# A hand-ordered delta-rule layer: its first four slots become an opening of their own

## The chip, the cores and the metric

The kernel runs on one core of one Trainium2 chip. The metric is the device time of one execution in microseconds (us); lower is better. Times given for a kernel are medians over several executions. The profile comes from one execution with the hardware profiler. The engines are called PE (TensorE, matmuls), ACT (ScalarE), DVE (VectorE), POOL (GpSimd) and SP (SyncE; here it issues nearly all DMAs).

## The reference

One layer in fp32 over 4 sequences of 1024 tokens with 512 features: a gated delta-rule attention with 16 heads of 128 by 128, and a mixture of experts (2 of 6 for each sequence, chosen by the sequence's mean). Both stand behind a layer norm and are added to their input.

```python
q = _l2norm(silu(short_conv(h @ Wq))) * SCALE      # conv over 4 tokens, per feature
k = _l2norm(silu(short_conv(h @ Wk)))
v = silu(short_conv(h @ Wv))
g = -exp(A_log) * softplus(h @ Wf1 @ Wf2 + dt_bias)   # 8 decay groups per head
beta = sigmoid(h @ Wb)

def step(S, inp):
    qt, kt, vt, gt, bt = inp
    S = S * exp(gt)[..., None]
    err = einsum('bhk,bhkv->bhv', kt, S)
    S = S + kt[..., None] * (bt[..., None] * (vt - err))[:, :, None, :]
    return S, einsum('bhk,bhkv->bhv', qt, S)

y = o * silu(h @ Wg + bg);  y = y * rsqrt(mean(y * y) + EPS) * norm_w
x = x + y @ Wo
x = x + moe(layernorm(x))
```

## The kernel before

**Tiling.** A sequence is cut into 4 blocks of 256 tokens (index j), a block into 2 chunks of 128; the 16 heads into 4 groups of 4. A *slot* is one sequence, head group and block: 64 slots, n = 16 b + 4 hg + j, of some 80 us each. A *unit* is one chunk of a slot. The recurrence is done by chunks: products of keys and queries inside a chunk, the inverse of a triangular matrix, then a chain over chunks that carries the state.

**The pieces of work.** They are Python generators; every `yield` ends a step.

- `norms(b, j)`: loads the block's two chunks of x (`xl`, L256), normalizes them (DVE `bn_stats`, POOL `rstd` L225/L226, DVE `xn` L227), transposes them on PE (`pt_a` L232) and copies them to `hT` on ACT (L233).
- `decays(b, j)`: PE `pf` (L272), ACT `f1T` (L276), PE `pbeta` (L281), ACT and DVE `beta` (L288 to L290), PE `pg` (L296), then a softplus over ACT and DVE (`gs`, `u`, `w`, L299 to L309) and a product on POOL (`gs`, L313).
- `factors_of(b, j)`: four PE products `px` (L324) of `gs`, each followed by an exponential on ACT into `xs` (L329) and a store of it into `fd` in device memory (L330). After the second and the fourth there is also a column `fgx` (L335), which goes out by four stores into `fg` (L338), one for each head group. At the end `pe` (L342), `xe` (L344) and a store into `fe` (L345). `f1T`, `u`, `w`, `xs` and `xe` share one tag of two buffers.
- `project(...)`: the q, k and v projections of a slot, in two parts of two heads. The weights are loaded with the first part (L358). For each head and each of q, k, v two half pieces of two PE products (`pz`, L400). ACT copies (`z`, L408) and does the first tap of the convolution (L410), DVE the others (L416, nine a head), ACT a Silu (L420).
- `front`: for each unit, loads `fx` from `fd` (L495), `eg` and `fe` (L500, L501), scales keys and queries with them on DVE (`kx` L521 to L532, `kq` L536), products on PE (`pin`, `pmid`, `pout`, L579), transposes (`pt` L620) and norms.
- `gate` (L666 to L675), `inverse` (L693 to L786: `pn` L705, `pxx` L723, `po` up to L782), `chain` (L801 to L845, with `pdl` L806) and `output` (L857 to L864), and for the experts `tokens`, `choose` and `experts`.

**Order.** PE's order is the order in which the program issues its instructions; the scheduler orders the other engines, with a priority for calls under `urgent`. `slot(n)` interleaves the chain of slot n (`c_`), the front of slot n + 1 (`f_`), the inverse of slot n + 1 (`i_`), dense work (`d`: outputs, gates, projections of slot n + 2) and extra work (`e_`) that `also(n, order, generator)` entered for the slot: norms, decays and factors of the coming blocks, and the experts. `fill(k)` takes k steps of the dense work. The twelve steps of the inverse are where `e_` is stepped, two times each, or once in slots with experts.

**The start.** Slots run from `first_slot = -4`; what `also` enters for an earlier slot is put into −4. Slots −4 to −1 have no chain. Slot −3 does the norms, decays and factors of block 0, with nothing beside them; slot −2 all the projections of slot 0, and then the norms, decays and factors of block 1; slot −1 the front of slot 0 (from its third step on), the projections of slot 1, the gate and the inverse of slot 0, and in the inverse's steps the norms, decays and factors of block 2.

A PE queue is worked off in order, so an instruction that waits holds all behind it; so are the queues of the other engines and SP's, where each DMA waits for the data that it stores or for the buffer that it fills.

Of the kernel before, what the change touches and what calls it, by code (L numbers as in the profile page):

```python
# [99 lines left out]
def layer_kernel(  # L100
# [25 lines left out]
    B, T, _ = x.shape  # L126
# [91 lines left out]
    def normed_rows(src, dst, who):  # L218

        st = sp.tile([P, 6], F32, tag="st", name=f"st_{who}")  # L220
        mv = sp.tile([P, 2], F32, tag="mv", name=f"mv_{who}")
        nc.vector.bn_stats(st, src)
        nc.vector.bn_aggr(mv, st)
        rstd = sp.tile([P, 1], F32, tag="rstd", name=f"rstd_{who}")
        nc.gpsimd.tensor_scalar(rstd, mv[:, 1:2], LN_EPS, None, ALU.add)  # L225
        nc.gpsimd.tensor_tensor(rstd, rstd, nhalf[:, :1], ALU.pow)  # L226
        nc.vector.tensor_scalar(dst, src, mv[:, 0:1], rstd[:, 0:1], ALU.subtract, ALU.mult)  # L227

    def transposed(xn, dst, who):
        pt = bank(f"pt_{who}", [P, KC, P])  # L230
        for kc in range(KC):
            nc.tensor.transpose(pt[:, kc, :], xn[:, kc * P : (kc + 1) * P], ident)  # L232
        nc.scalar.copy(dst, pt)  # L233


    def norms(b, j):
        if j == 0:
            seqs[b] = {
                "hT": {},
                "beta": bp.tile([P, NCH, H], F32, tag="beta", name=f"beta_{b}", bufs=2),  # L240


                "fg": dp.tile([NCH, NHG, NG, NH], F32, tag="fg", name=f"fg_{b}"),
                "fd": dp.tile([NCH, GW, NF * P], F32, tag="fd", name=f"fd_{b}"),

                "fe": dp.tile([NCH, P, GW], F32, tag="fe", name=f"fe_{b}"),

                "x1": dp.tile([NCH, P, D], F32, tag="x1", name=f"x1_{b}"),
                "xT": dp.tile([NCH, P, D], F32, tag="xT", name=f"xT_{b}"),
            }  # L250
        Q = seqs[b]
        xns = []
        for cc in range(CPB):
            c = j * CPB + cc
            xl = sp.tile([P, D], F32, tag="xr", name=f"xl_{b}_{c}", bufs=XR)
            nc.sync.dma_start(xl, x[b, c * P : (c + 1) * P, :])  # L256
            xn = sp.tile([P, D], F32, tag="xn", name=f"xn_{b}_{c}", bufs=3)
            normed_rows(xl, xn, f"a{b}_{c}")
            xns.append(xn)
        yield  # L260
        Q["hT"][j] = bp.tile([P, KC, TB], F32, tag="hT", name=f"hT_{b}_{j}", bufs=NBLK)
        for cc in range(CPB):
            transposed(xns[cc], Q["hT"][j][:, :, cc * P : (cc + 1) * P], f"a{b}_{j * CPB + cc}")
            yield

    def decays(b, j):
        Q = seqs[b]
        hT = Q["hT"][j]
        w_ = f"{b}_{j}"
        pf = bank(f"pf_{w_}", [P, TB])  # L270
        for kc in range(KC):
            nc.tensor.matmul(pf, wf1_sb[:, kc, :], hT[:, kc, :], start=(kc == 0), stop=(kc == KC - 1))  # L272
            if kc == 1:
                yield
        f1T = sp.tile([P, TB], F32, tag="xs", name=f"f1T_{w_}")
        nc.scalar.copy(f1T, pf)  # L276
        yield
        pbeta = bank(f"pbeta_{w_}", [P, CPB, H])
        for cc in range(CPB):
            for kc in range(KC):  # L280
                nc.tensor.matmul(  # L281
                    pbeta[:, cc, :], hT[:, kc, cc * P : (cc + 1) * P], wb_sb[:, kc, :],
                    start=(kc == 0), stop=(kc == KC - 1),
                )
            if cc + 1 < CPB:
                yield
        beta = Q["beta"][:, j * CPB : (j + 1) * CPB, :]
        nc.scalar.activation(beta, pbeta, AF.Exp, scale=-1.0)  # L288
        nc.vector.tensor_scalar(beta, beta, 1.0, None, ALU.add)
        nc.vector.reciprocal(beta, beta)  # L290
        yield

        gs = sp.tile([P, CPB, GW], F32, tag="gs", name=f"gs_{w_}", bufs=1)
        pg = bank(f"pg_{w_}", [P, CPB, GW])
        for cc in range(CPB):
            nc.tensor.matmul(  # L296
                pg[:, cc, :], f1T[:, cc * P : (cc + 1) * P], wf2_sb, start=True, stop=True,
            )
        nc.vector.tensor_add(gs, pg, dtb_sb[:, None, :].to_broadcast([P, CPB, GW]))  # L299
        u = sp.tile([P, CPB, GW], F32, tag="xs", name=f"u_{w_}")  # L300
        w = sp.tile([P, CPB, GW], F32, tag="xs", name=f"w_{w_}")
        nc.scalar.activation(u, gs, AF.Abs)
        nc.scalar.activation(u, u, AF.Exp, scale=-1.0)
        nc.vector.tensor_scalar(w, u, 1.0, None, ALU.add)

        nc.vector.scalar_tensor_tensor(u, w, -1.0, u, ALU.add, ALU.subtract)
        nc.scalar.activation(w, w, AF.Ln)
        nc.vector.tensor_sub(w, w, u)
        nc.vector.scalar_tensor_tensor(gs, gs, 0.0, w, ALU.max, ALU.add)  # L309
        gv = gs.rearrange("p c (h g) -> p (c h) g", g=NG)  # L310
        for cc in range(CPB):
            gv = gs[:, cc, :].rearrange("p (h g) -> p h g", g=NG)
            nc.gpsimd.tensor_tensor(gv, gv, nega[:, :, None].to_broadcast([P, H, NG]), ALU.mult)  # L313
        Q["gs"] = gs
        yield
# [732 lines left out]
    prs = [(b, hg, j) for b in range(B) for hg in range(NHG) for j in range(NBLK)]  # L1048
    parts = [list(range(i * NH // CPB, (i + 1) * NH // CPB)) for i in range(CPB)]
    NS = NHG * NBLK  # L1050
    begun = {}
    first_slot = -4
    sparse = set()
    beside = {}

    def also(n, order, g):
        beside.setdefault(max(n, first_slot), []).append((order, g))
# [10 lines left out]

    for b in range(B):
        for j in range(NBLK):  # L1070
            n = NS * b + j
            g = norms(b, j)
            also(n - 3, 1, some(g, 1))
            also(n - 3, 4, idle(2))
            also(n - 3, 5, g)
            also(n - 3, 6, idle(3))
            also(n - 3, 7, decays(b, j))
            also(n - 3, 8, idle(2))
            also(n - 3, 9, factors_of(b, j))
        for c in range(NCH):  # L1080
            also(NS * (b + 1) - NBLK + (c + 1) // 2, 0 if c % 2 else 3, tokens(b, c))
        n = NS * (b + 1) + 1
        also(n, 5, choose(b))
        g = experts(b)
        also(n, 8, some(g, 1))
        for c in range(NCH):
            also(n + 1 + c, 6, some(g, 4 * NFC + 1))
            sparse.add(n + 1 + c)
# [4 lines left out]
    def of(make, n, *k):  # L1093

        if not at(n):
            return iter(())
        b, hg, j = at(n)
        return make(b, hg, 2 * j + k[0]) if k else make(b, hg, j)

    def part(n, i):  # L1100
        return project(*at(n), parts[i]) if at(n) else iter(())

    def dense(n):
# [10 lines left out]
            yield  # L1114
        yield from part(n + 2, 1)

    def slot(n):
        d = dense(n)
        c_ = itertools.chain(of(chain, n, 0), of(chain, n, 1))
        f_ = begun.pop(n + 1, iter(()))  # L1120
        e_ = itertools.chain(*(g for _, g in sorted(beside.pop(n, []), key=lambda x: x[0])))

        def step(g):
            next(g, None)

        def urgent(g):

            with tc.high_priority(URGENT):
                next(g, None)

        def fill(k):
            for _ in range(k):
                next(d, None)

        step(f_)
        urgent(c_)
        fill(2)
        urgent(f_)
        fill(2)
        urgent(c_)  # L1140
        fill(1)
        urgent(f_)
        fill(1)
        urgent(f_)
        urgent(c_)
        fill(1)
        step(f_)
        urgent(c_)
        urgent(f_)
        fill(4)  # L1150
        urgent(c_)
        step(f_)
        fill(4)
        urgent(f_)
        fill(6)
        i_ = of(inverse, n + 1)
        for k in range(12):
            urgent(i_)
            fill(1 if k % 5 in (2, 4) else 2)
            for _ in range(1 if n in sparse else 2):  # L1160
                step(e_)
            if k in (0, 1, 3, 4, 9):
                urgent(c_)
            if k == 2:
                urgent(f_)
            if k == 5 and at(n + 2):
                begun[n + 2] = of(front, n + 2)
            if k in (5, 8) and at(n + 2):
                step(begun[n + 2])
        for g in (c_, f_, i_, d, e_):  # L1170
            for _ in g:
                pass

    with tc.manual_schedule(engines={mybir.EngineType.PE}):
        for n in range(first_slot, max(max(beside), len(prs)) + 1):
            slot(n)


# [46 lines left out]
```

## Time and profile before

| | |
|---|---|
| median of three executions | 5211.04 us (5199.04 to 5218.25) |
| profiled execution | 5219.7 us, its span 5217.9 us |
| mean granted clock of PE | 0.965 |
| PE busy | 4886.8 us, 94% |
| PE busy from 0 to 190 us | 126.05 us, at clock 0.81 |
| PE busy from 190 to 1000 us | 787.16 us, at clock 0.99 |
| DVE, ACT, POOL busy | 69%, 51%, 11% |

The span is the time from the profile's first to its last instruction. A profile line of a timeline reads: start, duration, engine, line of the program, operation, output<-input, shapes, how many instructions are drawn together, and in brackets how long the engine had been idle before and what released it. "PE px L324 <- POOL gs L313: 17.8, 3, 6.7" is a line of the waits: PE, at L324, waited for POOL's `gs` of L313 for 17.8 us in total, 3 times, 6.7 us at most. The windows view gives a stretch of time, its length, the busy time of PE, of its weight loads, of DVE, ACT and POOL with the number of instructions, the granted clock of PE (1.00 is full speed), the busy share of the DMA engines and GB/s.

In the profiled execution PE starts at 12.78 us, when the first `xn` is there. The slots' regular course, with PE nearly without idle time, sets in at some 190 us.

### The profile page before, as it was taken

How to read it: one execution, taken by the hardware profiler on the slowest of the kernel's cores; microseconds unless marked ns; L12 is line 12 of the kernel's file. 1: busy time of each engine (PE TensorE's matmuls, PEld its weight loads, DVE VectorE, ACT ScalarE, POOL GpSimd, SP SyncE). 2: the span in 40 equal slices, each digit the busy share in tenths (PEclk: the TensorE clock that was granted, in tenths of full speed). 3: DMA queues.
4: the chain of work that ended last, by engine and by line, in shares of the span. 5: the costliest groups of instructions: out<-in, count | busy, mean ns of one | idle time of the engine just before them, and what ended most of it. 6: DMA issues, size and time to landing. Idle time of an engine off the chain costs nothing.

```text
span 5217.9 us, 197872 instructions
## 1 busy us (share of the span) xinstructions
PE 4886.8 (94%) x86500; PEld 3683.3 (71%) x86500; DVE 3576.1 (69%) x10397; ACT 2676.3 (51%) x8111; POOL 555.9 (11%) x838
## 2 busy tenths in 40 slices
PE   6899999998899999998889999999888999999988
PEld 4677777776667777776667777777666777777765
DVE  4577878766676776776657667677765776677762
ACT  3445555554455555544455555555454555555531
POOL 1001111111110011101110100101111001001110
PEclk8899999999999999999989999999998999999999
DMA  5233433334344454434334545443533445444322
GB/s 140 64 102 102 108 102 108 100 83 102 98 115 127 116 158 115 128 96 102 100 84 116 137 123 141 121 118 101 118 84 89 127 132 140 128 125 129 82 59 73
DMA packets 333776, 573.01 MB, mean 110 GB/s; under 512 B 90022, under 2 KB 145190, under 8 KB 332908
## 3 DMA queue, kind: packets, MB, share of 16 engines
q1 hardware_dynamic: 332908, 560.34, 40.4%
q8 instruction: 678, 11.11, 1.0%
q14 instruction: 190, 1.56, 0.1%
HBM read 491.01 MB, written 69.22 MB: 107 GB/s over the span
## 4 chain that ended last, share of the span: by engine, by line
PE 68%; DVE 14%; ACT 8%; DMA 5%; issue 3%; POOL 1%; SPq 0%; another core or an unknown queue 0%; POOLq 0%; ACTq 0%; DVEq 0%
PE pz L400 22%; PE pw L860 6%; PE pgt L666 5%; PE ph L1026 3%; PE pn L705 3%; PE pxx L723 3%; PE pfo L1037 3%; PE pin L579 3%; DMA fx<-fd 3%; DVE qkv L416 3%; DMA fd<-xs 2%; DVE kx L527 2%; PE pmid L579 2%; PE pk L801 2%; PE pt L620 2%
## 5 line engine op out<-in xcount | busy, mean ns | idle before, releaser
L416 DVE SCALAR_TENSOR_TENSOR qkv<-z,conv_sb,qkv 128x256 f32<-128x256 f32 x2304 | 1027.2, 486 | 733.9 <-ACT qkv L410 706.8
L527 DVE TENSOR_TENSOR kx<-qkv,fx 128x384 f32<-128x384 f32 x1024 | 541.2, 550 | 68.9 <-ACT qkv L420 48.3
L400 PE MATMUL pz<-hT,wk 128*128 128x256 f32 x2048 | 576.4, 406 | 0.0
L400 PE MATMUL pz<-hT,wv 128*128 128x256 f32 x2048 | 542.6, 393 | 0.0
L860 PE MATMUL pw<-wo,yT 128*128 128x512 f32 x1024 | 517.7, 631 | 24.6 <-ACT xe L344 23.0
L400 PE MATMUL pz<-hT,wq 128*128 128x256 f32 x2048 | 537.8, 396 | 0.6 <-issue 0.6
L666 PE MATMUL pgt<-wg,hT 128*128 128x512 f32 x1024 | 504.3, 605 | 5.2 <-ACT xe L344 5.2
L408 ACT COPY z<-pz 128x512 f32<-128x512 f32 (+1 forms) x512 | 245.8, 480 | 482.2 <-PE pz L400 480.5
L521 DVE TENSOR_TENSOR kx<-qkv,fx 128x128 f32<-128x128 f32 x1792 | 431.8, 284 | 81.2 <-ACT qkv L420 36.3
L579 PE MATMUL pin<-kx 128*32 128x32 f32 x16384 | 408.8, 199 | 38.5 <-DVE U L614 24.0
L400 PEld LDWEIGHTS pz<-hT,wq 128*128 128x128 f32 x2048 | 372.0, 191 | 75.8 <-issue 29.7
L400 PEld LDWEIGHTS pz<-hT,wv 128*128 128x128 f32 x2048 | 369.1, 190 | 79.3 <-issue 21.5
L579 PEld LDWEIGHTS pin<-kx 128*32 128x32 f32 x16384 | 377.6, 112 | 55.1 <-DVE U L614 36.1
L400 PEld LDWEIGHTS pz<-hT,wk 128*128 128x128 f32 x2048 | 374.1, 195 | 52.9
L410 ACT ACTIVATE qkv<-z,conv_sb 128x256 f32<-128x256 f32 x768 | 362.4, 504 | 14.5
L835 ACT ACTIVATE y<-gt 128x128 f32<-128x128 f32 x512 | 157.4, 307 | 391.6 <-DVE gt L816 379.2
L579 PE MATMUL pmid<-qkv 128*32 128x32 f32 x4096 | 343.2, 198 | 14.8 <-issue 14.8
L837 POOL TENSOR_TENSOR ssy<-ssy,nhalf 128x4 f32<-128x4 f32 x128 | 149.7, 1170 | 1929.6 <-DVE ssy L836 1929.6
L579 PE MATMUL pmid<-kx,qkv 128*32 128x32 f32 x4096 | 344.9, 199 | 4.1 <-DVE kx L532 3.4
L536 DVE TENSOR_TENSOR kq<-qkv,fx 128x256 f32<-128x256 f32 x512 | 211.7, 422 | 156.4 <-DMA fx<-fd 82.1
L860 PEld LDWEIGHTS pw<-wo,yT 128*128 128x128 f32 x1024 | 190.6, 201 | 170.3 <-issue 136.8
L420 ACT ACTIVATE qkv<-qkv 128x768 f32<-128x768 f32 x256 | 215.6, 842 | 171.9 <-DVE qkv L416 169.5
(192 smaller groups left out, 10011.8 us busy)
## 6 DMA issues: line engine op xcount, KB each, us to landing
fx<-fd SPq DMA_DIRECT2D x512, 512.0 KB
we<-in_W_dram SPq DMA_DIRECT2D x192, 256.0 KB
x<-xr SPq DMA_DIRECT2D x128, 256.0 KB
xr<-x SPq DMA_DIRECT2D x96, 256.0 KB
we<-in_W_dram SPq DMA_DIRECT2D x96, 192.0 KB
wq<-in_Wq_dram SPq DMA_DIRECT2D x16, 1024.0 KB
wk<-in_Wk_dram SPq DMA_DIRECT2D x16, 1024.0 KB
wv<-in_Wv_dram SPq DMA_DIRECT2D x16, 1024.0 KB
```

The source lines that it names most:

```text
L400: nc.tensor.matmul(pz[:, s - ss_[0], :], weights["w" + "qkv"[s]][:, kc, h * DK : (h + 1) * DK], seqs[b]["hT"][blk][:, kc, :], start=(kc == ...
L408: nc.scalar.copy(z[:, ss_[0] : ss_[-1] + 1, 3:], pz)
L410: nc.scalar.activation(cv[:, s_, :], z[:, s_, 0:TB], AF.Copy, scale=taps[:, s_, 0:1])
L416: nc.vector.scalar_tensor_tensor(cv[:, s, :], z[:, s, k : k + TB], taps[:, s, k : k + 1], cv[:, s, :], ALU.mult, ALU.add,)
L420: nc.scalar.activation(cv, cv, AF.Silu)
L521: nc.vector.tensor_mul(later_half(kx[p][l][:, 0], half), later_half(q, half), later_half(f_[:, :, l, :], half))
L527: nc.vector.tensor_mul(kt[:, :n, 1, hh, :], k[:, hh, None, :].to_broadcast([P, n, P]), f_[:, hh, l0 : l0 + n, :],)
L536: nc.vector.tensor_mul(kq2[:, 2 * p + hh, :, :], qk[:, hh, 0:2, :], f_[:, hh, nl, None, :].to_broadcast([P, 2, P]))
L579: nc.tensor.matmul(o, l_, r_, start=True, stop=True, tile_position=(0, a))
L666: nc.tensor.matmul(pgt, hT[:, kc, c % CPB * P : (c % CPB + 1) * P], weights["wg"][:, kc, :], start=(kc == 0), stop=(kc == KC - 1),)
L835: nc.scalar.activation(y2, y[:, h, :], AF.Square, accum_out=ssy[:, h : h + 1])
L860: nc.tensor.matmul(pw, yT[:, h, :], weights["wo"][:, h, :], start=(h == 0), stop=(h == NH - 1))
```

## The change

Slots −4 to −2 are gone. A new function `opening` does the norms and decays of blocks 0 and 1 and the factors of block 0, and takes one step of slot 0's projections (half a piece: two products) after each of their steps; the rest of the projections follows. The first step of `norms(0, 1)`, which loads x and normalizes, comes before the decays of block 0; the first step of `front` of slot 0, which asks for `fx`, behind the factors of block 0. The slots begin with −1, and the factors of block 1 are entered there, ahead of the extra work for block 2. In slot −1 `fill` also takes a step of the extra work after each step of dense work, so that factors of block 1 and norms, decays and factors of block 2 come earlier than the inverse's steps.

```diff
-    first_slot = -4
+    first_slot = -1
...
     for b in range(B):
         for j in range(NBLK):
+            if b == 0 and j < 2:
+                continue
             n = NS * b + j
...
+    def opening():
+
+        d = itertools.chain(part(0, 0), part(0, 1))
+
+        def with_dense(g, k=1):
+            for _ in g:
+                for _ in range(k):
+                    next(d, None)
+
+        with_dense(norms(0, 0), 0)
+        one = norms(0, 1)
+        next(one)
+        with_dense(decays(0, 0))
+        with_dense(one)
+        with_dense(range(3))
+        with_dense(factors_of(0, 0))
+        begun[0] = of(front, 0)
+        next(begun[0])
+        with_dense(decays(0, 1))
+        with_dense(d)
+        next(begun[0])
+
     def slot(n):
...
         def fill(k):
             for _ in range(k):
                 next(d, None)
+                if n < 0:
+                    step(e_)
...
     with tc.manual_schedule(engines={mybir.EngineType.PE}):
-        for n in range(first_slot, max(max(beside), len(prs)) + 1):
+        opening()
+        also(-1, 0, factors_of(0, 1))
+        for n in range(-1, max(max(beside), len(prs)) + 1):
             slot(n)
```

In the built programs the two PE queues are the same again from the products of unit 2 on (`pout`, `pmid`, `pin` of L579, right behind the last `po` of slot 0's inverse, L782); the queues of ACT, SP and POOL are the same behind the corresponding places, and DVE's has a few neighbours exchanged. ACT's table loads go from 230 to 234. On SP's queue, `xl` of chunk 2 goes ahead of `wq`, and `xl` of chunk 3 ahead of `wk` and `wv`; `wo` and the first `xr` come before the first `fd` store; the two `fx` loads of unit 1's first half stand among the `fd` stores of block 1.

## The prediction

> **What bounds the kernel now.** I read the page's first part, then its chain, then TensorE's waits of the opening, then the timelines that carry them.
>
> ```profile
> PE 4886.8 (94%) x86500; PEld 3683.3 (71%) x86500; DVE 3576.1 (69%) x10397; ACT 2676.3 (51%) x8111; POOL 555.9 (11%) x838
> PE 68%; DVE 14%; ACT 8%; DMA 5%; issue 3%; POOL 1%; SPq 0%; another core or an unknown queue 0%; POOLq 0%; ACTq 0%; DVEq 0%
> ```
>
> TensorE (PE) is busy 94% of the span, so only its idle and half-clock time can be won. The windows view (window, its length, PE busy, the other engines, mean granted PE clock) shows where the opening stands:
>
> ```profile
> 0.00:190.00 190.00, 126.05 (x1576) 95.14 (x1577) 86.69 (x252) 77.24 (x197) 20.41 (x50) 0.81 0.43 111
> 190.00:1000.00 810.00, 787.16 (x15471) 600.62 (x15470) 622.87 (x1797) 413.48 (x1376) 86.28 (x121) 0.99 0.38 100
> ```
>
> Up to 190 us PE idles 64.0 us, and works at clock 0.81; behind it 97% busy at 0.99. Waits of PE up to 175 us (total, times, longest), and the row at 184 us:
>
> ```profile
> PE px L324 <- POOL gs L313: 17.8, 3, 6.7
> PE pf L272 <- ACT hT L233: 13.7, 2, 13.1
> PE pt_a L232 <- DVE xn L227: 12.8, 1, 12.8
> PE pgt L666 <- ACT xe L344: 5.2, 1, 5.2
> PE pn L705 <- DVE xn L698: 5.0, 1, 5.0
> ...
> 184.03 1.33 PE L620 MATMUL pt<-cst,qkv 128*128 128x128 f32 x5 [6.12 <-ACT qkv L420]
> ```
>
> 17.8 + 13.7 + 12.8 + 5.2 + 5.0 + 6.1 = 60.6; four small ones make 3.4 more: the 64.0. The timelines of PE and ACT (start, duration, idle before and its releaser) place them:
>
> ```profile
> 27.39 6.32 PE L324 MATMUL px<-cst,gs 128*128 128x512 f32 x8 [5.98 <-POOL gs L313]
> 54.71 1.04 PE L232 MATMUL pt_a<-cst,xn 128*128 128x128 f32 x8
> 68.80 3.78 PE L272 MATMUL pf<-hT,wf_sb 128*128 128x256 f32 x8 [13.05 <-ACT hT L233]
> 83.51 5.56 PE L324 MATMUL px<-cst,gs 128*128 128x512 f32 x8 [6.66 <-POOL gs L313]
> ...
> 25.48 1.28 ACT L329 ACT_TABLE_LOAD   x1
> 39.89 0.60 ACT L329 ACTIVATE xs<-px 128x512 f32<-128x512 f32 x1 [6.25 <-DMA fd<-xs]
> 45.91 0.38 ACT L344 ACTIVATE xe<-pe 128x256 f32<-128x256 f32 x1 [3.06 <-DMA fd<-xs]
> 101.27 0.38 ACT L344 ACTIVATE xe<-pe 128x256 f32<-128x256 f32 x1 [10.54 <-DMA fd<-xs]
> ```
>
> The reader is to see two kinds of wait. Steps of norms and decays have nothing beside them on PE (5.98, 13.05, 6.66). And `xe` waits for the `fd` store that frees its `xs` buffer, because four tiny `fg` stores (0.1 KB each, L338) stand ahead of it: the DMA records have the first `fg` issued at 32.26 and the next `fd` landed at 45.89; 88.37 and 101.17 in the second block. I call these 12.8 to 13.6 us the tail.
>
> Half clock is the other loss. The clock records show it over 22.45–32.69, 59.99–87.30, 100.95–107.78, 128.26–141.91, 158.98–165.81 and 182.87–189.70; PE is busy in 5.3 + 11.8 + 6.1 + 11.0 + 6.5 + 5.7 = 46.4 us of that, and half, 23, is excess. The first transposes and `pf` (1.97 and 3.76 us, against 1.04 and 1.73 later) add 3. So 26.
>
> **The change part by part.** PE's work is the same; its queue and the old one are the same again from the products of unit 2 on, right behind `po` L782 (ends at 173.95 before). I walk the new queues, each wait by the rows above, up to `pdl` L806 (ends at 190.0 before), the first place behind the 6.12.
>
> *Pieces between block 0's steps.* Half pieces of slot 0's projections (1.73 us for a whole one) now lie between `pf`, `pbeta` and `pg`, so `pg` ends at 25.05 instead of 21.4. ACT and DVE need 7.0 us from there to `gs` (5.98 before, and norms of block 1 now beside them): 32.05. The pieces on PE last until 31.1. Idle 0.95 instead of 5.98. On SP's queue `xl_2` now goes before `wq`, and `xl_3` (which waits for `xn`, 12.75) before `wk` and `wv`: they are issued at about 13.1 instead of 8.26 and 8.80. At the rate of before (1 MB in 2.5 us) wq, wk, wv land at 16.3, 19.5, 22; the pieces reach wk at about 21. Hidden, with 1.5 us in hand; past that, each us costs one.
>
> *Block 1's `hT`.* 13.05 us before, since its copies stood in ACT's queue behind slot 0's convolutions (Silu at 61.82, then 65.38). Now they come before most of these: 0.
>
> *Factors of block 0.* `xs` come later (first `fd` issued at 36.85, 30.12 before), the first `fg` at 38.4, so by the tail the store lands at 51.2 and `xe` runs at 52.6 behind a table load (1.28). Behind `xe` on ACT stands the copy of `f1T` for block 1 (L276), and `pg` of block 1 waits for it: idle 47.3 to 54.4, 7.1 us, new. PE's pieces behind `pg` wait too.
>
> *Factors of block 1, in slot −1.* `px` at 71.1 after 4.0 us. The second `fx` load of unit 1 now stands on SP between two `fd` stores and waits for `kq` (L536): `fd` at 79.0, so the last `px` and `pe` wait 3.5. Together 7.5 against 6.66. `xe` runs at 96 (101.27 before); a `pz` piece is behind it, idle 6.3 against 5.2.
>
> *Block 2 ahead of the inverse.* The extra step in `fill` brings block 2's `px` from 159.35 to before `pn` (L705). `pg` ends at 114.85; 6.66 us as in block 1, and a table load, a Silu (1.28, 0.84) and DVE's pair work in between, put `gs` at 125.25: idle 10.4 against 5.1. In PE's queue the whole inverse stands behind it, so `pn`'s own 5.0 is covered. Nearest rows: 5.1 below, and above the 22.9 us from 101.7 to 124.6 in which DVE is 84% busy; I keep 10.4, by block 1. Its `xe` (144.7) then holds ACT, and `pn` for 16 waits 3.3, new.
>
> *`pt` L620.* Its Silu comes some 20 us before it is needed: 6.1 to 0.
>
> Idle after: 12.8 + 0.7 (start, unchanged) + 0.95 + 7.1 + 7.5 + 6.3 + 10.4 + 3.3 + 3.4 (small, unchanged) = 52.4; **11.6 us less**. Half clock after: in before it sets in 4 to 5 us into an idle stretch and stays some 6 us of work, so the idles of 7.1, 6.3 and 10.4 cost 3 each, with 3 at the start 12; **14 less**. Table loads go from 230 to 234; by the row 4 x 1.28 = 5.1 us of ACT, which is half idle here, and two of them are inside the sums above.
>
> In the Trainium skill, "ScalarE: Activation LUTs", What ACT_TABLE_LOAD costs, a switch is 1283 ns plus a drain of about 1380. The trace agrees with the first; at 25.48 the load follows its predecessor at once, so no drain shows. By the page's 2.66 us the four would be an estimated 10.6 us and, if all lay on the path, the gain 5.5 less.
>
> In the skill's "TensorE: Matmul & The Clock Gate", Part 1, the warm-up takes "~3.4 µs of time". Here half clock lasted 4 to 12 us after work resumed (0.55 mean from 68.8 to 89.4). By the page an estimated 1.7 us of excess per idle instead of 3, and a gain 4 us larger.
>
> **Sum.** 25.6 us at `pdl`. From there the queues are those of before and PE is 97% busy, so it is carried to the end: 5219.7 − 25.6 = 5194.1 for the profiled execution. The median of the three runs is 5211.04, 0.9983 of that execution: **5186 us**. One half per cent, about what a measurement of this kernel can tell from no change, is 26 us, so the forecast lies on that line.
>
> **Rivals.**
> 1. *The tail is shorter than I take it* (0.25). In the first block a 1 MB load of `wo` (landed 39.08) shared it, and after the change `wo` is out of the way. Then the waits behind `xe` of blocks 0 and 1 go: 7.1 + 6.3 + 6 of half clock, gain 45, **5166**. Against it: the second block's tail, with no such load, was 12.8.
> 2. *The tail is longer* (0.13), since `fx` loads (512 KB) now lie among the `fg`: three waits 3 to 4 us longer, 12 in all, gain 13.6, **5197**.
> 3. *The change doesn't do what it says* (0.04): `hT` of block 1 or the weights stay late, and 13.05 with 4 of half clock comes back; gain 8, **5203**.
> 4. *The gain is eaten behind 190 us* (0.04) by the 22.8 us of idle up to 1000, if they hang on something that did not move; **5211**. Every queue moved alike, which is against it.
> 5. *Slower* (0.07): block 2's `px` ahead of the inverse. All of PE waits for one `gs` whose DVE steps stand behind the fronts' work. If PE drains and DVE does its whole backlog first, the wait is not 10.4: from 36 us on the gain is gone, at 45 the time is **5220**. For it: DVE 84% busy there. Against: 45 is twice that window.
>
> **How the numbers follow.** The forecast has 0.47, for gains of 15 to 36 (5175 to 5196): each wait is good to some 3 us. Just over half of it, 0.25, and rival 1 lie beyond 26 us: faster 0.50. The rest, 0.22, with rivals 2, 3 and 4 (0.21): same 0.43. Rival 5: slower 0.07. The range takes in rivals 1 to 3 with the spread of the runs (5199 to 5218): 5160 to 5210.
>
> **What would show it.** Right: no 13 us wait for `hT`; `px` of block 0 at 32 with under 2 us idle; `pg` of block 1 waiting for `f1T` until 54; a 10 us wait for `gs` at 125, before `pn`; no wait at the `pt` of 184; `pdl` ending at 164. Wrong: a `pz` that waits for a weight before 25 us; `fd` landing under 8 us behind the first `fg`; a wait over 20 us for block 2's `gs`; or `pdl` 25 us early and an end that is not.

## The result and the profile after

| | before | changed |
|---|---|---|
| median, 20 executions each | 5214.64 us | 5200.85 us (5193.70 to 5212.43) |
| ratio to before, 95% interval | | 0.9977, 0.9971 to 0.9984 |
| span of the profiled execution | 5217.9 us | 5191.9 us |
| end of `pdl` (L806) in it | 190.16 us | 172.03 us |
| PE busy / idle up to there | 126.21 / 63.95 us | 117.29 / 54.74 us |

By the ratio the change is faster by 0.23%, 12.0 us (8.3 to 15.1), where 25.6 had been forecast. Below are the windows views up to the end of `pdl`, first of the kernel before, then of the changed one (window, length, PE busy, then PE's weight loads, DVE, ACT, POOL, the granted clock):

```profile
0.00:190.16 190.16, 126.21 (x1577) 95.30 (x1578) 86.69 (x252) 77.40 (x197) 20.41 (x50) 0.81 0.43 112
```

```profile
0.00:172.03 172.03, 117.29 (x1577) 88.23 (x1578) 87.74 (x252) 81.47 (x200) 20.03 (x50) 0.86 0.46 122
```

The number of matmuls is the same, 1577, so the two rows can be subtracted: 9.2 us less idle, 8.9 us less busy for the same work. PE's waits in the changed kernel up to there, and the places in its timeline:

```profile
PE pt_a L232 <- DVE xn L227: 13.2, 1, 13.2
PE px L324 <- POOL gs L313: 11.0, 3, 9.9
PE pe L342 <- ACT fgx L335: 10.3, 1, 10.3
PE pg L296 <- ACT f1T L276: 6.9, 1, 6.9
PE pout L579 <- DVE kx L527: 2.6, 1, 2.6
```

```profile
32.63 1.12 PE L324 MATMUL px<-cst,gs 128*128 128x512 f32 x2 [0.74 <-POOL gs L313]
54.99 1.23 PE L296 MATMUL pg<-wf_sb,f1T 128*128 128x128 f32 x4 [6.92 <-ACT f1T L276]
...
92.28 1.22 PE L342 MATMUL pe<-gs,cst 128*128 128x128 f32 x4 [10.29 <-ACT fgx L335]
...
128.53 2.08 PE L324 MATMUL px<-cst,gs 128*128 128x512 f32 x2 [9.91 <-POOL gs L313]
```

The 13 us wait for `hT` and the 6.1 at `pt` are gone, and `px` of block 0 waits 0.74 instead of 5.98. New are the wait for `f1T`, which stands on ACT behind `xe` of block 0, the 10.29 in front of `pe` of block 1, and 9.91 for block 2's `gs`. ACT shows what holds `pe` and `f1T`:

```profile
52.20 1.28 ACT L344 ACT_TABLE_LOAD   x1 [7.44 <-DMA fd<-xs]
91.56 0.60 ACT L329 ACTIVATE xs<-px 128x512 f32<-128x512 f32 x1 [9.94 <-DMA fd<-xs]
```

Both wait for an `fd` store. By the DMA records the first was issued at 41.21 and landed at 52.13, behind four `fg` stores that were begun at 38.25; the second was issued at 79.92, behind two `fx` loads and ahead of four `fg` stores, and landed at 91.48.

How far one pair of profiles can be trusted is seen from three more profiles, two of the changed kernel and one of the kernel before: PE's lead, matmul by matmul counted from the end, at four places of the run.

| pair | at 237 us | at 2277 | at 4443 | at the end |
|---|---|---|---|---|
| before, changed | 15.6 | 12.4 | 31.2 | 25.9 |
| before, before again | −0.4 | −1.2 | 8.5 | 2.0 |
| before, changed again | 9.5 | 6.9 | 18.7 | 18.1 |
| before again, changed a third time | 13.7 | 16.8 | 21.1 | 22.0 |

The lead out of the opening differs by up to 6 us between profiles of the changed kernel. Behind 2400 us the kernel before drifts by 8.5 us against itself, and the two first profiles of the changed kernel, 6.1 us apart at 237 us, are 12.5 apart at 4443. So the 26 us between the first pair's spans are not all the change's. The leads at 237 us lie about the 12.0 us that the ratio gives.

### The profile page after: what moved, and what is told of

The parts are those of the page before. It is cut to its first block, busy times and chain, and to the rows that moved or that the text cites. A ratio compares the mean times of both kernels' runs of the same rounds, so it can differ in the third digit from the quotient of the medians.

```text
span 5191.9 us, 197876 instructions
## 1 busy us (share of the span) xinstructions
PE 4873.6 (94%) x86500; PEld 3676.3 (71%) x86500; DVE 3577.5 (69%) x10397; ACT 2681.0 (52%) x8115; POOL 558.7 (11%) x838
## 4 chain that ended last, share of the span: by engine, by line
PE 67%; DVE 15%; ACT 8%; DMA 5%; issue 3%; POOL 1%; SPq 0%; another core or an unknown queue 0%; POOLq 0%; ACTq 0%; DVEq 0%
PE pz L400 22%; PE pw L860 6%; PE pgt L666 5%; PE ph L1026 3%; PE pn L705 3%; DMA fx<-fd 3%; PE pxx L723 3%; PE pin L579 3%; PE pfo L1037 3%; DVE qkv L416 3%; DVE kx L527 2%; PE pmid L579 2%; PE pk L801 2%; PE pt L620 2%; PE pdl L806 2%
## 5 line engine op out<-in xcount | busy, mean ns | idle before, releaser
L579 PE MATMUL pin<-kx 128*32 128x32 f32 x16384 | 414.5, 200 | 44.9 <-DVE U L614 23.6
L579 PEld LDWEIGHTS pin<-kx 128*32 128x32 f32 x16384 | 382.9, 113 | 60.6 <-DVE U L614 36.0
L579 PE MATMUL pmid<-kx,qkv 128*32 128x32 f32 x4096 | 347.7, 200 | 7.2 <-issue 4.4
L579 PE MATMUL pmid<-qkv 128*32 128x32 f32 x4096 | 346.6, 199 | 3.1 <-issue 3.1
```

Source lines behind the costliest of these rows:

```text
L579: nc.tensor.matmul(o, l_, r_, start=True, stop=True, tile_position=(0, a))
```

## The experiments

Each ran beside executions of the kernel before on the same chip; the ratio is to those. "pdl" is the end of `pdl` (L806, or the line that it has there) in the profile: 190.2 and 189.6 in two profiles of the kernel before, 172.0 in the changed one.

| run | pdl | PE busy / idle to there | ratio | 95% interval |
|---|---|---|---|---|
| after2 | 176.5 | 119.1 / 57.4 | 0.9970 | 0.9958 to 0.9982 |
| after3 | 174.3 | 118.9 / 55.3 | one run | |
| before2 | 189.6 | 125.3 / 64.3 | one run | |
| a_fxpool | 176.0 | 118.8 / 57.2 | 0.9984 | 0.9972 to 0.9996 |
| a_fgpool | 185.2 | 120.7 / 64.5 | 0.9975 | 0.9963 to 0.9986 |
| a_b2late | 178.5 | 122.3 / 56.2 | 0.9985 | 0.9974 to 0.9995 |
| b_fill | 180.2 | 121.4 / 58.8 | 0.9981 | 0.9971 to 0.9991 |
| a_plain | not used | | 0.9960 | 0.9945 to 0.9975 |
| a_plain2 | 184.5 | 124.6 / 59.9 | 0.9979 | 0.9970 to 0.9988 |
| b_fgrow | 167.9 | 121.1 / 46.9 | 0.9769 | 0.9756 to 0.9782 |
| a_fgrow | 149.5 | 112.3 / 37.2 | 0.9732 | 0.9719 to 0.9744 |
| a_row4 | 151.8 | 113.7 / 38.1 | 0.9750 | 0.9726 to 0.9774 |
| a_plainrow | 159.2 | 116.4 / 42.8 | 0.9767 | 0.9754 to 0.9780 |
| a_b2row | 160.9 | 121.4 / 39.5 | 0.9748 | 0.9735 to 0.9761 |
| a_rowidle | 143.7 | 111.0 / 32.6 | 0.9731 | 0.9718 to 0.9744 |

### The changed kernel again

> The changed kernel once more, beside the others of this call. All theories: ratio 0.997 to 0.9985, pdl ends at 171 to 173.

> The changed kernel again, for a third profile of its opening: pe of block 1 waits 10 to 14 us, pdl ends at 171 to 177. If the forecast's 3.5 us was only unlucky: below 6 us and 168.

> The kernel before again, for a second profile of its opening. If the waits behind the fg stores are of steady length: pdl ends at 189 to 191. If they vary by several us, as between the two profiles of the changed kernel (172.0 and 176.5): anywhere from 186 to 195.

`pe` of block 1 waited 13.13 and 8.86 us (the second is below the 10 to 14 expected), so the 10.29 was no accident, and `pdl` ends at 172.0, 176.5 and 174.3, on average 15.6 us ahead of the kernel before. after2 missed its 173. Its ratio agrees with the first.

### Are the fx loads in SP's queue the cause?

```diff
-                nc.sync.dma_start(
+                (nc.gpsimd if p == 1 and (b, hg, c) == (0, 0, 1) else nc.sync).dma_start(
                     fx[p][:, hh].rearrange("p l t -> p (l t)"),
```

> The changed kernel, with the two fx loads of unit 1 (its second half, 512 KB each) issued from POOL's queue, so that on SP's queue no fx load stands between the fd stores of block 1. Theory A (most of what the gain fell short of the forecast was lost at the second fd store of block 1, which stood behind these loads): that store lands within 4 us of its issue instead of 11.6, pe of block 1 starts by 86 instead of 92.3, and pdl ends 5 to 7 us earlier than in the changed kernel (172.0), at 165 to 167; ratio to the kernel before 0.9962 to 0.9968. Theory B (the shortfall lies in block 2's px ahead of the inverse): the wait for gs before px of block 2 grows by what pe wins, pdl ends at 171 to 173, ratio 0.9977.

Half of theory A came true: the second `fd` store landed 2.0 us after its issue, and `pe` did not wait. But nothing was won. PE's waits of this run:

```profile
PE px L324 <- POOL gs L313: 11.0, 3, 9.9
PE pz L400 <- ACT xe L344: 10.6, 1, 10.6
PE pg L296 <- ACT f1T L276: 6.6, 1, 6.6
```

The wait went from `pe` to the next in the queue that needs an `xs` buffer: the third `fd` store, issued at 79.59 behind the four `fg` stores and beside the two `fx` loads, landed at 98.32. Besides, PE stood still for 6.2 us at `pn` without a semaphore that explains it. Theory A fell; theory B's longer wait for `gs` did not come either (9.9, as in the changed kernel). Here the late landing was moved and not shortened.

### Is the tail in SP's queue, in the number of stores, or in their elements?

```diff
-                        nc.sync.dma_start(Q["fg"][c, hg].rearrange("g (h o) -> h g o", o=1), fgx[r, :])
+                        nc.gpsimd.dma_start(Q["fg"][c, hg].rearrange("g (h o) -> h g o", o=1), fgx[r, :])
```

> The changed kernel with all fg stores issued from POOL's queue, in all 16 blocks. If the tail behind a set of fg stores belongs to SP's own DMA queue: the fd stores that follow land within 4 us of their issue; pg of block 1 waits under 3 us instead of 6.9, pe of block 1 some 4 instead of 10.3 (the fx loads ahead of it stay), pdl ends 8 to 12 us earlier, at 160 to 164, ratio 0.9955 to 0.9960, with more if later blocks wait for it too. If the fg elements fill the DMA engines themselves, whatever queue they come from: the tails stay at 10 us and more, and the ratio is 0.9975 to 0.9980.

It isn't SP's queue: the third `fd` store was issued at 40.74 with no `fg` store ahead of it there, and landed at 53.56. The wait at `pg` fell to 2.2 us, but PE stood still for 7.0 us at `pn` without a semaphore that explains it, and two waits behind `fd` are longer or new:

```profile
PE pe L342 <- ACT fgx L335: 11.9, 1, 11.9
...
PE pz L400 <- ACT xe L344: 8.2, 1, 8.2
```

`pdl` ended 9 to 13 us later than in the changed kernel; the ratio shows nothing of that.

In the Trainium skill, "DMA: Bandwidth & Descriptors", Rules for kernel authors, a non-contiguous last dimension "lowers to one descriptor per element", and spreading DMAs over issuing engines doesn't help since they run on the same DMA engines. This run agrees with the second. The next runs agree with the first: with the 4096 elements of their column stores, 4544 DMA packets go away (333776 to 329232). They turn the column to a row on PE, once in a chunk, and store that:

```diff
+        def rows():
+            while held:
+                c, fgx = held.pop()
+                pr = bank(f"pr_{b}_{c}", [P, GW])
+                nc.tensor.transpose(pr[:1, :], fgx[:GW, :], ident)
+                fgr = sp.tile([P, NHG, NG, NH], F32, tag="fgr", name=f"fgr_{b}_{c}", bufs=2)
+                nc.scalar.copy(fgr[:1], pr[:1, :].rearrange("o (a h g) -> o a g h", a=NHG, g=NG))
+                nc.sync.dma_start(Q["fg"][c, None], fgr[:1])
...
+                rows()
                 xs = sp.tile([P, 4, P], F32, tag="xs", name=f"xs_{b}_{c}_{f0}")
...
-                    for hg in range(NHG):
-                        r = slice(hg * NH * NG, (hg + 1) * NH * NG)
-                        nc.sync.dma_start(Q["fg"][c, hg].rearrange("g (h o) -> h g o", o=1), fgx[r, :])
+                    held.append((c, fgx))
...
+        rows()
         xe = sp.tile([P, CPB, GW], F32, tag="xs", name=f"xe_{b}_{j}")
```

> The changed kernel, with the column fgx turned to a row by one PE transpose and an ACT copy, and stored into fg as one row of 512 bytes instead of four stores of 4-byte elements. Theory C: no tail is left: each fd store lands within 4 us of its issue (up to 8 behind fx loads), the 6.9 us of pg and the 10.3 us of pe go or fall under 3, pdl ends 12 to 18 us earlier, at 154 to 160, and later blocks win their waits of output and gate for xe (16.7 us in all); ratio 0.990 to 0.9945. Rival (the tail comes from the fx loads of 512 KB, or from the many DMAs at once): waits of 6 us and more for fd stay, ratio 0.9965 to 0.998.

> The kernel before with the same row store of fg. Theory C: xe of blocks 0 and 1 no longer wait 3 and 10.5 us, pgt's 5.2 and some half clock are won, 6 to 9 us at the opening, and the waits for xe later (23 us in all): ratio 0.994 to 0.9975. The change is then worth more on top of it than alone: the ratio of the changed kernel with the row store lies 0.0025 to 0.005 below this one. Rival: ratio 0.999 to 1.001.

Theory C held, and by far more than its numbers: 2.7% on the changed kernel, 2.3% on the kernel before. On top of the row store the change is worth 0.0037 of the ratio (0.9769 to 0.9732), inside the 0.0025 to 0.005 expected. In the opening of a_fgrow the third `fd` store was issued at 40.57 and landed at 43.18. Its waits, with the gs waits left and all of those behind `fd` gone or under 3 us:

```profile
PE px L335 <- POOL gs L313: 14.1, 3, 9.9
PE pt_a L232 <- DVE xn L227: 13.4, 1, 13.4
PE pr L326 <- ACT xe L355: 2.6, 1, 2.6
PE pr L326 <- ACT fgx L347: 1.5, 3, 0.8
PE pz L411 <- ACT hT L233: 1.5, 1, 1.5
```

One wait behind an `fd` store is left in the opening of b_fgrow, 6.1 us at `pr` for `fgx`: a store issued at 32.29, ahead of any `fg` store, landed at 40.24, beside the 1 MB load of `wo` (30.96 to 39.52). The same store of the kernel before (31.83 to 39.78) holds ACT for the 6.25 us at 39.89; so of block 0's waits there, that one is not the work of `fg`.

I had priced only the waits that name `xe`. From the kernel before to b_fgrow the profiled span fell by 108.7 us, of which 33.7 are busy time of PE (4886.8 to 4853.1). PE's waits over the whole run, first before, then b_fgrow:

```profile
PE pw L860 <- ACT xe L344: 23.0, 7, 5.2
PE pt L620 <- ACT qkv L420: 18.0, 5, 6.1
PE pmid L579 <- issue: 15.3, 5, 5.2
...
PE pin L579 <- issue: 12.2, 7, 5.6
```

```profile
PE pmid L590 <- issue: 5.7, 4, 2.0
...
PE pin L590 <- issue: 2.3, 2, 1.9
```

The waits for `xe` are no longer listed. The waits that no semaphore explains ("issue") fell from 27.5 to 8.0 us at these two places, and from 46.2 to 19.9 in all. Of the seven such waits over 4 us in the kernel before, one, at `ph`, is in b_fgrow too; the other six begin 0.2 to 14.5 us behind an `fg` store, and b_fgrow has no other over 2.1 us. So they go with these stores; what PE lacks there, the views do not tell.

To tell the number of stores from the size of their elements, a_row4 stores the row by four DMAs:

```diff
-                nc.sync.dma_start(Q["fg"][c, None], fgr[:1])
+                for hg in range(NHG):
+                    nc.sync.dma_start(Q["fg"][c, hg, None], fgr[:1, hg])
```

> The changed kernel with the row of fg stored by four DMAs of 32 neighbouring elements (128 bytes) each, so as many DMAs as in the changed kernel, in the same places, but no elements of 4 bytes. If the elements make the tail: fd stores land within 4 us (8 behind fx loads), pdl ends at 149 to 152, ratio 0.9725 to 0.974, as with one DMA. If the number of small DMAs makes it: waits of 6 us and more for fd remain, pdl ends at 165 or later, ratio above 0.985.

The `fd` store right behind four such DMAs landed 2.06 us after its issue (43.55 to 45.61). So it is the 4-byte elements and not the number of stores; whether their reading from 32 partitions or their writing takes the time, the runs do not separate. `pdl` was as expected; the ratio, with a wide interval, is a little above.

### What do the parts of the change bring?

The pieces between the steps of the opening, taken out (with the first half piece ahead of `begun`, which needs its tiles):

```diff
-        def with_dense(g, k=1):
+        def with_dense(g, k=0):
...
+        next(d)
         begun[0] = of(front, 0)
...
-        with_dense(d)
+        for _ in d:
+            pass
```

> The changed kernel with no pieces of projections between the steps of norms, decays and factors of the opening: they all follow behind the decays of block 1. If the interleaving is what wins: gs of block 0 is waited for 6 us instead of 0.74, xe and f1T waits lie bare (7 or more) and PE starts the pieces some 15 us later; pdl ends at 185 to 190, ratio 0.9995 to 1.0005. If the new order of blocks alone wins (norms of both blocks first), pdl ends by 176 and the ratio is below 0.9985.

> The changed kernel without pieces of projections between the steps of the opening, again, for its profile. Theory C (what is left of the opening's idle time hangs on the tail behind the fg stores, and the pieces only move where PE meets it): PE waits for gs of block 0 and 1 bare (6 and 3 to 6 us), but xe of block 0 and f1T of block 1 come while 24 pieces are still to do, so the 6.9 us wait and its half clock are gone; pdl ends within 3 us of the changed kernel, ratio within 0.0010 of it. Theory D (the interleaving wins the gain): pdl ends 10 us or more behind the changed kernel, at 182 or later, and the ratio is 0.002 above it.

> The changed kernel with the row store of fg and with no pieces of projections between the steps of the opening. Theory D (the pieces win part of the gain, tail or not): PE waits bare for gs of block 0 (6) and meets half clock behind it, pdl ends 7 to 11 us behind that of the changed kernel with the row store (149.5), at 156 to 161; ratio 0.9745 to 0.9755. Theory C (the pieces only move where PE meets the tail): without a tail pdl is within 3 us of 149.5 and the ratio within 0.0008 of 0.9732.

The first of these runs gave no usable profile, so it was made again. By the openings theory D holds: `pdl` ends 8 to 12.5 us later without the pieces, and 9.7 later where there is no tail. The ratios agree only in the second case (0.9767 against 0.9732); in the first the intervals overlap, 0.9960 lies even below the changed kernel's, and the ratios can't tell.

The step in `fill` alone, on the kernel before, and the changed kernel with block 2 left in the inverse:

```diff
                 next(d, None)
+                if n < 0:
+                    step(e_)
```

> The kernel before with one part of the change alone: in the slots below 0, fill takes a step of the extra work with each dense step; four opening slots as before. hT of block 1 and its gs then lie among slot 0's projections (13.05 and 6.66 gone), and block 2's px come ahead of the inverse; gs of block 0 stays bare (5.98). If the order of blocks 1 and 2 is most of the change's worth: pdl ends at 172 to 178, ratio 0.997 to 0.9982. If the opening's own order is: pdl ends at 183 or later, ratio 0.999 or more.

```diff
                 if n < 0:
-                    step(e_)
+                    next(lead, None)
...
-        also(-1, 0, factors_of(0, 1))
+        lead = factors_of(0, 1)
```

> The changed kernel, in which slot -1 takes only the factors of block 1 with its dense steps; norms, decays and factors of block 2 are stepped in the inverse, as in the kernel before. Theory A: the 9.9 us wait for block 2's gs goes, but pn waits for its xn (5.0 before) and px of block 2 for gs behind the inverse (5.1 before), both with half clock: pdl ends within 3 us of 172.0, ratio 0.9975 to 0.9980. Theory B: 9.9 us and half clock of some 4 are won and little comes back; pdl ends by 163, ratio 0.9960.

> The changed kernel with the row store, and with norms, decays and factors of block 2 back in the inverse's steps. If placing block 2 ahead of the inverse costs (9.9 us wait for gs): pdl ends at 140 to 145, ratio 0.971 to 0.972. If it pays, as the run with the four stores showed (178.5 against 172 to 176.5): waits for xn before pn, for gs and for qkv before pt come back, pdl ends at 150 to 156, ratio 0.9735 to 0.9745.

b_fill alone wins 10 us at `pdl` (180.2, between its two forecasts); the change without block 2's move wins 11.4; both together 15.6. With the row store, block 2's move is worth 11.4 (160.9 against 149.5). The intervals of their ratios overlap, so only the openings can tell. Theory B was wrong twice; theory A of a_b2late, within 3 us of 172.0, was missed as well, and a_b2row ends behind its 156. `px` of block 2 ahead of the inverse does wait 9.9 us, but in the inverse `pn` and `px` wait 6.6 and 5.1 us, and `pt` 6.3. With the row store the idle time of the two differs by only 2.3 us: the other 9.1 are busy time of PE, and 8.5 of these come from half clock (30.6 us of work at half clock in a_b2row, 13.6 in a_fgrow). The wait can be had cheaper:

```diff
-            also(n - 3, 8, idle(2))
+            also(n - 3, 8, idle(2 if n > 2 else 14))
```

> The changed kernel with the row store, and with 12 idle steps more before the factors of block 2, so that pg of block 2 stays ahead of the inverse and px comes after the inverse's first two products of L705 (no work added). If the 9.9 us wait for gs is only a matter of place: the inverse's first steps run in it, px waits under 3 us, pdl ends at 140 to 146, ratio 0.971 to 0.9725. If what waits moves to the inverse's own chain (pn for xn, DVE busy with the pair work): pdl ends at 148 to 150, ratio 0.973 to 0.974.

The longest wait for `gs` falls from 9.9 to 3.5 us:

```profile
PE px L335 <- POOL gs L313: 4.2, 2, 3.5
PE pn L716 <- DVE xn L709: 3.2, 1, 3.2
```

`pdl` ends at 143.7, 46 us ahead of the kernel before. The ratio, 0.9731, is the lowest of all, though not clear of a_fgrow's. This version beats both kernels by 2.5 to 2.7%.

## Why the prediction was wrong in size

The way was right: each stall that was to go went, and the time fell. The size was wrong: 25.6 us forecast against 12.0 (the median, 5200.85, lies inside the range), and three terms of the sum were off.

**The half-clock term, "14 less".** It was the largest error: PE's busy time fell by 8.9 us (7.1 and 7.3 in the two other profiles). The step that failed is "the idles of 7.1, 6.3 and 10.4 cost 3 each, with 3 at the start 12". The clock records of the changed kernel show five stretches of half clock behind the start, not three:

```profile
51.20:58.10 6.90, 3.11 (x9) 2.71 (x10) 3.79 (x11) 3.68 (x10) 0.00 (x0) 0.51 0.79 77
64.90:75.10 10.20, 8.48 (x115) 5.59 (x115) 8.83 (x24) 7.18 (x13) 1.06 (x2) 0.50 0.58 143
85.40:95.60 10.20, 3.32 (x109) 3.10 (x110) 2.40 (x6) 0.88 (x3) 0.00 (x0) 0.50 0.15 52
119.50:133.20 13.70, 4.67 (x68) 2.28 (x69) 8.37 (x29) 7.85 (x15) 1.00 (x2) 0.50 0.28 65
140.00:146.80 6.80, 4.92 (x72) 3.63 (x72) 1.10 (x2) 0.27 (x1) 0.00 (x0) 0.50 0.19 43
```

PE is busy in them for 24.5 us, half of which, 12.3, is excess (13.6 in each of the two other profiles), where the sum had 9. The three that were foreseen, the first, third and fourth, cost 1.6, 1.7 and 2.3 us and so less than 3 each. The second and the fifth, 4.2 and 2.5 us, were not foreseen at all: in the 3.41 us ahead of them PE is idle for 2.97 and 1.58 us in all, and the longest idles there are 2.61 us (DVE's `kx` late for the products) and 1.15.

So what I had read from the kernel before, that half clock sets in 4 to 5 us into an idle stretch, was wrong. Its own first row says otherwise: idle from 21.41, half clock from 22.45. And the fourth stretch of the changed kernel begins 0.9 us into the 9.91 us wait, in the third profile even 0.8 us ahead of that wait (118.36 and 119.12).

The start took 3.3 us where the sum had 3. By this reckoning the excess falls from 26 to 15.6, so 10.4 us; the measured 8.9 leave 1.5 us of busy time that are not explained.

The Trainium skill, "TensorE: Matmul & The Clock Gate", Part 1, tells of free-running activity windows of 3413 ns. The trace agrees: the five stretches are two, three, three, four and two times 3.41 us long. No run here varied what falls into one window alone, so what makes the clock drop stays open.

**The idle term, "11.6 us less".** It was 9.2 (6.6 and 8.6 in the others). The walk placed nearly every wait that it had: `px` of block 0 at 32.63 for 32.05, `pg` at 54.99 for 54.4, `gs` of block 2 9.91 for 10.4, `pt` none. Two came out shorter: block 1's `gs` 0.35 for 4.0, and `pn` for 16 0.6 for 3.3.

"`fd` at 79.0, so the last `px` and `pe` wait 3.5", and then 6.3 at a `pz` behind `xe`, came as one wait of 10.29 (13.13, 8.86) at `pe`: 9.8 forecast in two places. There the tail was laid on stores issued behind the `fg` alone; the store at 79.92 was issued ahead of them, and landed 11.6 us later all the same. In a_fgrow and a_row4 the store in its place, behind the same two `fx` loads, landed 5.6 and 5.9 us after its issue, so about half of the 11.6 goes with these loads and half with the column.

What failed in this term is "3.4 (small, unchanged)": 4.3 us for `kx`, 1.5 for `hT` and 5.5 that no semaphore explains came in their place. These last are no work of the change alone: they are 6.1 and 6.4 us in the other profiles of the changed kernel, 0.6 and 6.3 in the two of the kernel before, and 1.1 in a_fgrow.

**The carry, "so it is carried to the end".** Of 15.6 us at `pdl` (mean of the profiles) some 13 are left at 237 us. With the chain reached earlier, `pyt` (L843) waits 3.5 us for ACT's `gt`, 0.9 at most before. In the first pair, up to the matmul at 237 us, there are 1.9 us more idle time and 0.8 us more busy time behind `pdl`, with half clock from 184.37 to 187.78. From 237 us to 2277 the lead changes by 3 us one way or the other, and the ratio has it.

Of the rivals, the longer tail (13.6) gave the number, but not by its mechanism: the waits behind `fd`, 20.2 us in the forecast (7.1 + 3.5 + 6.3 + 3.3), were 15.8 to 19.6. The shorter tail, the late `hT`, and the slower outcome are excluded by the profile; of a gain eaten behind 190 us there is only the part named under the carry. The median inside the range is no support for the sum: the range was wide enough for a gain of 1 us. The tail was read rightly as the cause of `xe`'s waits, and then taken for given; without it either kernel is 2.3 to 2.7% faster, ten times what the change brings.

## What to carry to other kernels

When a walk through the queues gives the waits well, cost the clock with the same care: write down the idle of each few microseconds, not only the long gaps. A wait that is moved past its cause comes back at the next instruction that needs the same buffer; look at what makes the transfer late before its place in a queue is changed. A store whose elements lie apart is small only in bytes: see how long the next transfer takes to land.

## What was not expected of the hardware

A 256 KB store among eight stores of 32 elements of 4 bytes landed 10.9 us after its issue (41.21 to 52.13) where these came from SP's queue, and 12.8 us where they came from POOL's; right behind rows of 128 or 512 bytes it landed 2.1 to 2.6 us after its issue. Without such stores the whole run was 2.3 to 2.7% shorter, though only 1.4% of the DMA packets went away (329232 instead of 333776). And PE's clock was halved after an idle of 2.6 us followed by short products: PE was busy for 0.44 of the 3.41 us ahead of 64.90.
